# Softplus of a Mamba block by ScalarE's own function, in place of abs, relu, exp and ln summed by matmuls

## The chip, the cores and the metric

The kernel runs on one core of a Trainium2 chip. The metric is the device time of one execution in microseconds (us), as the median of the runs. A core has five engines that work side by side, each on its own instructions in their own order: TensorE (PE in the profile, with its weight loads as PEld), VectorE (DVE), ScalarE (ACT), GpSimd (POOL) and SyncE (SP), which here only issues transfers (DMAs). Engines wait for one another by semaphores. Tensors lie in SBUF; matmuls write to PSUM, which has eight banks of 128 partitions x 512 fp32 values.

## The reference

The input is 64 channels x 256 times x 128 frequencies. Layer 0 is a bidirectional Mamba block, first along time (128 sequences of 256), then along frequency (256 sequences of 128), each with a forward and a backward direction `d`. Layer 1 is a convolutional LSTM. The change concerns `dt` of layer 0, which is the same in all four blocks (2 stages x 2 directions):

```python
x = silu(conv(x) + conv_b)
dt, Bm, Cm = split(x @ x_proj_w.T)
dt = softplus(dt @ dt_proj_w.T + dt_proj_b)
h = exp(dt * A) * h + dt * B * x      # scan over the sequence
y = (sum over states of h * C + x * Dp) * silu(z)
```

`dt` has 128 values (the inner channels) per token. There are 16 states per channel, so `h` has 2048 rows per token.

## The kernel before

A stage (`class Stage`) works through 64 chunks of 512 tokens; the two stages make 128 chunks. A chunk has 16 steps S (`run`, L686): for each direction eight steps, each with 2 x 128 of the 2048 rows of h, that is, 128 partitions x 1024 values. One step consists of

- `inputs` (L546): two products on TensorE that spread dt times x over the states into the tile `bx` (two PSUM banks, three such tiles), issued two steps ahead of the scan;
- `decays` (L561): ScalarE's exp of dt times A into `dA` (four buffers), also two steps ahead;
- `times_b` (L580): `bx` times B, on VectorE, or on GpSimd for the "swapped" steps 2, 5, 9 and 14 of each chunk, for which ScalarE has copied `bx` to `dA` (L570) and put the exp into `bx`;
- `recur` (L590): the scan, on VectorE;
- `outputs` (L608): h times C, on GpSimd;
- `add_up` (L613): in every second step, four matmuls on TensorE that fold the states into `y`, two steps behind the scan.

The order of the work is written out by hand: each engine executes its instructions in the order in which `run` issues them. Within a step S that order is: times_b(S+1), recur(S), gate, outputs(S-1), inputs(S+2), decays(S+2), then what the tables `HEAD` (from chunk 1) or `SECOND` (chunk 0) put at slot S, then skip and add_up(S-2) with the closing of the last chunk, then what they put at S + 0.5.

These tables say when the preparations for the next chunk are done: loading, the norm (`means`, `rms`, `normalise`), the projections of x and z with the short convolution (`project_x`, `project_z`), `silus`, `dt`, `B` and `C`. Slots are steps of the chunk under way; slot 16 is step 0 of the new chunk itself. At slot 5, `project_x` of direction 1 is followed by `silus`: ScalarE loads the table set of silu (L385), applies silu to x and z of both directions (L389) and loads the table set of exp and ln again (L390). Around it `decays` is issued for two steps at slot 5 and for none at slot 6 (L707).

All small matmul results of a stage (px, pz, pb, pv, pm, po, made) take turns in one single PSUM bank, the tile with the tag "mm" (`mm`, L301): a new one is written only when the former has been read.

Softplus before is max(v, 0) + log(1 + exp(-|v|)) in three parts. `softplus_a` (L392) has the product `pv` and, on ScalarE, Abs into e, Relu within pv and exp into e. `softplus_b` (L405) takes w = e + 1, its Ln, and 1 - w. `softplus_sum` (L414) adds e, 1 - w and lw to pv by three matmuls with the identity, since 1 - w corrects the rounding of e + 1; ScalarE copies the sum to `dt`. The bank is held from softplus_a to that copy. `dt_away` (L426) then writes dt to DRAM by four DMAs on SP's queue, from where `spread_dt` (L456) fetches it for each step, spread over the states, into seven buffers; `times_x` (L433) makes dt times x on GpSimd. `first` (L471) does all that for the first chunk of a stage, before the steps begin.

Of the kernel before, what the change touches and what calls it, by code (L numbers as in the profile page):

```python
# [29 lines left out]
F32 = mybir.dt.float32  # L30
BF16 = mybir.dt.bfloat16
AF = mybir.ActivationFunctionType
# [4 lines left out]
P = 128  # L37
# [9 lines left out]
NTOK = 512  # L47
# [15 lines left out]
SWAPPED = (2, 5, 9, 14, 18, 21, 25, 30)  # L63
EXP_AND_LN = "natural_log_exp_and_others"
SILU = "silu_and_others"
EDGES = (0, 1, LF - 2, LF - 1)


# [10 lines left out]
    (5, "project_x", 1),  # L79
    (5, "silus"),  # L80
    (7.5, "project_bc", 0),
    (8, "softplus_a", 0),
    (8.5, "softplus_b", 0),
    (8.5, "spread_bc", 0, 0),
    (10.5, "softplus_sum", 0),
    (10.5, "dt_away", 0),
    (11.5, "times_x", 0),
    (12, "spread_bc", 0, 1),
    (12, "spread_dt", 0, 0),
    (12, "spread_dt", 0, 1),  # L90
    (12.5, "project_bc", 1),
    (12.5, "spread_dt", 0, 2),
    (13, "softplus_a", 1),
    (13, "softplus_b", 1),
    (13.5, "spread_dt", 0, 3),
    (14.5, "spread_dt", 0, 4),
    (15, "softplus_sum", 1),
    (15.5, "dt_away", 1),
    (16, "spread_dt", 0, 5),
    (16.5, "spread_dt", 0, 6),  # L100
    (16.5, "spread_dt", 0, 7),
# [15 lines left out]
SECOND = tuple(  # L117
    (max(slot, 16), *step) for slot, *step in HEAD if step[0] == "spread_dt" and step[1:] > [0, 3]
) + (
    (14, "softplus_a", 1),  # L120
    (15, "softplus_b", 1),
    (15, "softplus_sum", 1),
    (15, "dt_away", 1),
    (16, "spread_bc", 1, 0),
    (16, "spread_bc", 1, 1),
# [4 lines left out]
class Mamba:  # L130
# [58 lines left out]
    def load(self, first):  # L189
        dma, d = self.nc.sync.dma_start, self.d  # L190
        if first:
            dma(out=self.win[:, 0], in_=d["in_proj"][:, 0])
            dma(out=self.cw[:, 0], in_=d["conv_w"][0].partition_broadcast(C))
            dma(out=self.cols, in_=d["cols"])
            dma(out=self.xdt, in_=d["dt_proj"])
            dma(out=self.Wbc, in_=d["x_proj_bc"])
        else:
            dma(out=self.win[:, 1:4], in_=d["in_proj"][:, 1:4])
            dma(out=self.cw[:, 1:4], in_=d["conv_w"][1:4].partition_broadcast(C))
            dma(out=self.lin, in_=d["lin_w"])  # L200
            dma(out=self.b, in_=d["lin_b"])
            dma(out=self.ow, in_=d["out_proj"])
# [55 lines left out]
class Stage:  # L258
# [98 lines left out]
    def shifted(self, px, i):  # L357
        nc, m, L = self.nc, self.m, self.L
        first, second = (3, 1) if i % 2 == 0 else (4, 6)
        nc.tensor.matmul(self.seqs(px), lhsT=m.G1[i], rhs=self.unp[:, :, first : first + L], start=True, stop=False)  # L360
        nc.tensor.matmul(self.seqs(px), lhsT=m.G2[i], rhs=self.unp[:, :, second : second + L], start=False, stop=True)  # L361
# [21 lines left out]
    def silus(self, ch):  # L383
        nc = self.nc
        nc.scalar.preload_act_table_set(SILU)  # L385
        for n in ("xs", "zs"):
            for d in range(2):
                t = self.at[n, ch, d]
                nc.scalar.activation(t, t, AF.Silu)  # L389
        nc.scalar.preload_act_table_set(EXP_AND_LN)  # L390

    def softplus_a(self, ch, d):  # L392


        nc, m, wk = self.nc, self.m, self.wk
        i = 2 * self.stage + d
        pv = self.mm("pv")
        nc.tensor.matmul(pv, lhsT=m.Wdt[i], rhs=self.at["xs", ch, d], start=True, stop=True)  # L398
        e = wk.tile([P, NTOK], F32, name="e", tag="e")
        nc.scalar.activation(e, pv, AF.Abs, bias=m.dtb[:, i : i + 1])  # L400
        nc.scalar.activation(pv, pv, AF.Relu, bias=m.dtb[:, i : i + 1])
        nc.scalar.activation(e, e, AF.Exp, scale=-1.0)  # L402
        self.at["e", d], self.at["pv", d] = e, pv

    def softplus_b(self, ch, d):  # L405
        nc, wk = self.nc, self.wk
        w = wk.tile([P, NTOK], F32, name="w", tag="w")
        lw = wk.tile([P, NTOK], F32, name="lw", tag="lw")
        nc.scalar.activation(w, self.at["e", d], AF.Identity, bias=1.0)
        nc.scalar.activation(lw, w, AF.Ln)  # L410
        nc.scalar.activation(w, w, AF.Identity, scale=-1.0, bias=1.0)  # L411
        self.at["w", d], self.at["lw", d] = w, lw

    def softplus_sum(self, ch, d):  # L414

        nc, pv = self.nc, self.at["pv", d]
        parts = [self.at[n, d] for n in ("e", "w", "lw")]
        for n, t in enumerate(parts):
            nc.tensor.matmul(  # L419
                pv, lhsT=self.m.ident, rhs=t, start=False, stop=n == len(parts) - 1, skip_group_check=True  # L420
            )
        dt = self.wk.tile([P, NTOK], F32, name="dt", tag="dt", bufs=2)
        nc.scalar.copy(dt, pv)  # L423
        self.at["dt", d] = dt

    def dt_away(self, ch, d):  # L426

        there = self.dram.tile([32, 2, 2, NTOK], F32, name="there", tag="there")
        for r in range(4):
            self.nc.sync.dma_start(out=there[:, r % 2, r // 2], in_=self.at["dt", d][32 * r : 32 * r + 32])  # L430
        self.at["there", ch, d] = there

    def times_x(self, ch, d):  # L433
        dtx = self.wk.tile([P, NTOK], F32, name="dtx", tag="dtx", bufs=3)
        self.nc.gpsimd.tensor_mul(dtx, self.at["dt", d], self.at["xs", ch, d])  # L435
        self.at["dtx", ch, d] = dtx

    def project_bc(self, ch, d):
# [32 lines left out]
    def first(self):  # L471


        nc, m = self.nc, self.m
        s, time = 2 * self.stage, self.time
        banks = [self.ps_bx.tile([P, 2, NTOK], F32, name="bx", tag="bx") for _ in range(3)]
        self.load(0)
        if time:
            m.load(True)
        self.squares(0)  # L480
        if time:
            m.shifts(0)
        self.means(0)
        self.rms(0)
        nc.scalar.preload_act_table_set(SILU)
        self.normalise_here()
        if time:
            m.dt(0, self.mm("pw"))
            m.load(False)
        x, z = {}, {}  # L490
        for d in range(2):
            x[d] = self.wk.tile([P, NTOK], F32, name="xs", tag="xs", bufs=3)
            z[d] = self.wk.tile([P, NTOK], F32, name="zs", tag="zs", bufs=4)
            self.at["xs", 0, d], self.at["zs", 0, d] = x[d], z[d]
        self.shifted(banks[0][:, 0], s)
        nc.scalar.activation(x[0], banks[0][:, 0], AF.Silu, bias=m.cb[:, s : s + 1])
        nc.scalar.preload_act_table_set(EXP_AND_LN)
        self.softplus_a(0, 0)
        if time:
            m.decay()  # L500
            m.spreads()
            m.gates(0)
            m.shifts(1)
            m.gates(1)
        self.softplus_b(0, 0)
        self.spare = [banks[0][:, 1]]
        self.project_bc(0, 0)
        self.spread_bc(0, 0, 0)
        self.softplus_sum(0, 0)
        self.dt_away(0, 0)  # L510
        self.times_x(0, 0)
        for n in range(4):
            self.spread_dt(0, 0, n)
            if n == 0:
                self.spread_bc(0, 0, 1)
        if time:
            m.dt(1, self.mm("pw"))
        self.shifted(banks[1][:, 0], s + 1)
        for d in range(2):
            self.gated(banks[1 + d][:, 1], s + d)  # L520
        nc.scalar.preload_act_table_set(SILU)
        nc.scalar.activation(x[1], banks[1][:, 0], AF.Silu, bias=m.cb[:, s + 1 : s + 2])
        for d in range(2):
            nc.scalar.activation(z[d], banks[1 + d][:, 1], AF.Silu)
        nc.scalar.preload_act_table_set(EXP_AND_LN)
        self.spare = [banks[2][:, 0]]
        self.project_bc(0, 1)
        if time:
            m.folds(self.mm("pf"))
            for i in (2, 3):  # L530
                m.shifts(i)
                m.gates(i)
                m.dt(i, self.mm("pw"))
            for n in range(2):
                m.residual(n)
            for i in range(4):
                m.closing(i, self.mm("pc"))
# [274 lines left out]
class ConvLstm:  # L812
# [35 lines left out]
    def prepare(self):  # L848
        nc, tc, X, d, acc = self.nc, self.tc, self.X, self.d, self.acc
        g = self.gates.gb[:, 0:1]  # L850
        with tc.tile_pool(name="l_prep", bufs=1) as wp, tc.tile_pool(
# [28 lines left out]
            def border(wts, e, half, qs):  # L880

                tiles = []
                for gate in range(2):
                    pe = ps.tile([P, HALF, 2], F32, name="pe", tag="pe")
                    for q in qs:
                        x = EDGES[e] + q - 2
                        nc.tensor.matmul(  # L887
# [148 lines left out]
    def convolve_a(self, group, pair):  # L1036
# [6 lines left out]
        for e in range(2):  # L1043
            nc.scalar.copy(
                pre[:, :, :, EDGES[2 * e] : EDGES[2 * e] + 2],
                self.gxe[:, 2 * pair : 2 * pair + 2, half, rows, 2 * e : 2 * e + 2],
# [216 lines left out]
```

## Time and profile before

| | |
|---|---|
| time, median of 3 runs | 7332.51 us (7311.43 to 7338.29) |
| profiled execution, first to last instruction | 7324.0 us |
| stage along time, then along frequency, by the trace | about 0 to 3260 us and 3260 to 6550 us |
| ConvLSTM, by the trace | about 6550 us to the end |
| VectorE busy | 6924.8 us (95%) |
| GpSimd busy | 6703.3 us (92%) |
| TensorE busy | 6510.4 us (89%) |
| ScalarE busy | 6119.2 us (84%) |
| DMA engines busy, mean from 100 to 3200 us | 84% |

A line of the profile's groups names the code line (L598 is line 598), the engine, the operation, the tile written and the tile read, their shapes and the number of instructions; then the busy time in us, the mean of one instruction in ns, and the time that the engine stood idle just before such instructions, with what ended most of that. A line of the timeline has the start in us, the duration, the engine, the line and the operation with its count; what stands in brackets at its end is the idle time before it and the instruction whose end released it. Instructions of one engine overlap by about 0.1 us, and fp32 matmuls are shown in two passes.

### The profile page before, as it was taken

The page shows a single profiled execution, that of the slowest core. Times are in us where ns is not written, and L with a number is a line of the kernel's source. Part 1 is how long each engine was busy: PE and PEld are TensorE (multiplying, and loading weights), DVE is VectorE, ACT ScalarE, POOL GpSimd, SP SyncE. Part 2 cuts the span into 40 slices and gives each one's busy share as a digit, 9 for nine tenths or more (in the row PEclk, how much of TensorE's full clock was granted, in tenths as well). Part 3 has the DMA queues.
Part 4 walks back from the last instruction along what each step waited for, and adds up shares of the span by engine and source line. Part 5 has one row for each costly group of instructions (what it writes and reads, how often), then busy time and mean ns, then how long its engine had stood idle before and what let it go on. Part 6 is the DMA issues. An engine that isn't in the chain of part 4 may idle for free. (4 is left out here: it accounts for less than half of the span.)

```text
span 7324.0 us, 86482 instructions
## 1 busy us (share of the span) xinstructions
PE 6510.4 (89%) x25104; PEld 2254.8 (31%) x25104; DVE 6924.8 (95%) x4684; ACT 6119.2 (84%) x11092; POOL 6703.3 (92%) x3410
## 2 busy tenths in 40 slices
PE   8888888888888888887898898888888888888999
PEld 2222222222222222222222222222222222226887
DVE  7999999999999999997999999999999999996887
ACT  7888889888898888987999999988998989983333
POOL 6999999999999999997999999999999999995554
PEclk9999999999999999999999999999999999999999
DMA  7888888888888888886888888878888788882000
GB/s 171 206 206 208 199 210 204 205 207 205 210 203 209 206 204 207 204 210 159 208 211 209 210 215 200 208 197 202 206 201 204 199 209 198 205 202 62 15 15 17
DMA packets 505887, 1359.47 MB, mean 186 GB/s; under 512 B 72772, under 2 KB 129732, under 8 KB 505416
## 3 DMA queue, kind: packets, MB, share of 16 engines
q1 hardware_dynamic: 505416, 1353.93, 74.6%
q8 instruction: 205, 3.36, 0.2%
q14 instruction: 266, 2.18, 0.1%
HBM read 1228.34 MB, written 92.27 MB: 180 GB/s over the span
## 5 line engine op out<-in xcount | busy, mean ns | idle before, releaser
L611 POOL TENSOR_TENSOR h<-h,C 128x1024 f32<-128x1024 f32 x2048 | 4797.5, 2366 | 32.4 <-DVE h L598 22.0
L598 DVE TENSOR_TENSOR_SCAN h<-dA,bx 128x1024 f32<-128x1024 f32 x1536 | 3443.8, 2269 | 0.0
L553 PE MATMUL bx<-dtx,sel 64*128 64x512 f32 x8192 | 2578.7, 653 | 364.8 <-DVE h L598 362.5
L588 DVE TENSOR_TENSOR bx<-bx,B 128x1024 f32<-128x1024 f32 x1536 | 1863.7, 1213 | 178.8 <-PE bx L553 178.2
L576 ACT ACTIVATE dA<-rep,cols 128x510 f32<-128x510 f32 (+1 forms) x3072 | 2021.7, 710 | 11.3 <-DMA rep<-there 11.3
L585 POOL TENSOR_TENSOR dA<-dA,B 128x1024 f32<-128x1024 f32 x512 | 1205.9, 2355 | 161.9 <-ACT dA L570 155.8
L553 PEld LDWEIGHTS bx<-dtx,sel 64*128 64x128 f32 x8192 | 733.3, 190 | 1888.1 <-issue 1070.5
L620 PE MATMUL y<-h,fold 128*32 128x512 f32 x8192 | 1239.5, 618 | 12.6 <-POOL h L611 10.9
L598 DVE TENSOR_TENSOR_SCAN h<-bx,dA 128x1024 f32<-128x1024 f32 x512 | 1167.9, 2281 | 15.4 <-POOL dA L585 15.4
L570 ACT COPY dA<-bx 128x1024 f32<-128x1024 f32 x512 | 518.5, 1013 | 352.7 <-PE bx L553 338.0
L576 ACT ACTIVATE bx<-rep,cols 128x510 f32<-128x510 f32 (+1 forms) x1024 | 705.5, 689 | 33.7 <-ACT bx L573 0.4
L398 PE MATMUL pv<-xs,wdt 128*128 128x512 f32 x512 | 341.2, 753 | 261.5 <-ACT bc L443 167.5
L620 PEld LDWEIGHTS y<-h,fold 128*32 128x32 f32 x8192 | 188.5, 109 | 933.5 <-issue 504.0
L435 POOL TENSOR_TENSOR dtx<-dt,xs 128x512 f32<-128x512 f32 x256 | 327.6, 1280 | 54.2 <-ACT dt L423 33.7
L364 PE MATMUL pz<-unp,wz 64*128 64x512 f32 x504 | 283.5, 642 | 91.0 <-ACT X L669 54.0
L360 PE MATMUL px<-unp,g 128*128 128x512 f32 x504 | 283.8, 644 | 9.5 <-DMA unp<-xn 7.0
L419 PE MATMUL pv<-e,ident 128*128 128x512 f32 x512 | 288.1, 645 | 3.4 <-ACT e L402 3.4
L441 PE MATMUL pb<-xs,wbc 128*32 128x512 f32 x504 | 260.9, 599 | 15.6 <-ACT made L809 15.6
L419 PE MATMUL pv<-w,ident 128*128 128x512 f32 x512 | 262.6, 594 | 6.1 <-ACT w L411 6.1
L419 PE MATMUL pv<-lw,ident 128*128 128x512 f32 x512 | 262.3, 594 | 0.0
L361 PE MATMUL px<-unp,g 128*128 128x512 f32 x504 | 257.8, 592 | 0.0
L1150 POOL TENSOR_TENSOR y<-v,X 128x512 f32<-128x512 f32 x32 | 40.6, 1270 | 230.7 <-DVE v L1148 230.7
(206 smaller groups left out, 7066.0 us busy)
## 6 DMA issues: line engine op xcount, KB each, us to landing
rep<-there SPq DMA_DIRECT2D x2048, 512.0 KB, 7.8
B<-away SPq DMA_DIRECT2D x256, 256.0 KB, 8.9
there<-dt SPq DMA_DIRECT2D x1024, 64.0 KB, 3.3
C<-away SPq DMA_DIRECT2D x256, 256.0 KB, 3.4
unp<-xn SPq DMA_DIRECT2D x504, 64.0 KB, 3.3
away<-bc SPq DMA_DIRECT2D x256, 64.0 KB, 4.1
u<-in_x SPq DMA_DIRECT2D x128, 64.0 KB, 8.9
out<-y SPq DMA_DIRECT2D x32, 256.0 KB, 2.0
```

The costliest lines, as they stand in the source:

```text
L360: nc.tensor.matmul(self.seqs(px), lhsT=m.G1[i], rhs=self.unp[:, :, first : first + L], start=True, stop=False)
L398: nc.tensor.matmul(pv, lhsT=m.Wdt[i], rhs=self.at["xs", ch, d], start=True, stop=True)
L419: nc.tensor.matmul(pv, lhsT=self.m.ident, rhs=t, start=False, stop=n == len(parts) - 1, skip_group_check=True)
L435: self.nc.gpsimd.tensor_mul(dtx, self.at["dt", d], self.at["xs", ch, d])
L553: self.nc.tensor.matmul(bx[:, j], lhsT=self.m.sel[rows, r, k], rhs=dtx[rows], start=True, stop=True)
L570: nc.scalar.copy(dA.rearrange("p j n l -> p j (n l)"), bx)
L576: nc.scalar.activation(dA[:, j, :, live], self.seqs(rep[:, j])[:, :, live], AF.Exp, scale=m.A[:, i, g : g + 1])
L585: self.nc.gpsimd.tensor_mul(bx, bx, b)
L588: self.nc.vector.tensor_mul(bx, bx, b)
L598: self.nc.vector.tensor_tensor_scan(h.rearrange("p j n -> p (j n)")[:, step], dA[:, step], bx[:, step], 0.0, ALU.mult, ALU.add,)
L611: self.nc.gpsimd.tensor_mul(h, h, self.at["C", ch, d].unsqueeze(1).to_broadcast([P, 2, NTOK]))
L620: nc.tensor.matmul(y[32 * r : 32 * r + 32], lhsT=m.fold[:, k], rhs=hs[r % 2][:, r // 2], start=False, stop=k == NK - 1, skip_group_check=True,
```

## The change

Softplus becomes one ScalarE function, read from PSUM with the bias and written to `dt`. It needs a table set of its own, "softplus". For all chunks but a stage's first, both directions are done within `silus`, at slot 5: the product pv of direction 0 (`step_size`) is issued behind the silu of its x; after the four silus come the load of the new table set, `softplus` of direction 0, the product pv of direction 1, its softplus, and the load of the exp and ln set. The steps softplus_a, softplus_b and softplus_sum leave the tables; `dt_away` moves from slots 10.5 and 15.5 (15 in chunk 0) to 8 and 14.5 (15 in chunk 0, as before). `dt` gets three buffers in place of two. In `first`, the softplus of direction 0 and what follows from it come right behind its silu, with a table load more, and direction 1 is done behind the silus of the second half.

```diff
@@ HEAD
     (5, "project_x", 1),
     (5, "silus"),
     (7.5, "project_bc", 0),
-    (8, "softplus_a", 0),
-    (8.5, "softplus_b", 0),
     (8.5, "spread_bc", 0, 0),
-    (10.5, "softplus_sum", 0),
-    (10.5, "dt_away", 0),
+    (8, "dt_away", 0),
     (11.5, "times_x", 0),
...
     (12.5, "project_bc", 1),
     (12.5, "spread_dt", 0, 2),
-    (13, "softplus_a", 1),
-    (13, "softplus_b", 1),
     (13.5, "spread_dt", 0, 3),
     (14.5, "spread_dt", 0, 4),
-    (15, "softplus_sum", 1),
-    (15.5, "dt_away", 1),
+    (14.5, "dt_away", 1),
@@ SECOND
-    (14, "softplus_a", 1),
-    (15, "softplus_b", 1),
-    (15, "softplus_sum", 1),
     (15, "dt_away", 1),
@@ silus
                 nc.scalar.activation(t, t, AF.Silu)
+                if n == "xs" and d == 0:
+                    self.step_size(ch, 0)
+        nc.scalar.preload_act_table_set(SOFTPLUS)
+        self.softplus(ch, 0)
+        self.step_size(ch, 1)
+        self.softplus(ch, 1)
         nc.scalar.preload_act_table_set(EXP_AND_LN)
 
-    def softplus_a(self, ch, d):
...
-    def softplus_b(self, ch, d):
...
-    def softplus_sum(self, ch, d):
...
+    def step_size(self, ch, d):
+        i = 2 * self.stage + d
+        self.at["pv", d] = pv = self.mm("pv")
+        self.nc.tensor.matmul(pv, lhsT=self.m.Wdt[i], rhs=self.at["xs", ch, d], start=True, stop=True)
+
+    def softplus(self, ch, d):
+        i = 2 * self.stage + d
+        dt = self.wk.tile([P, NTOK], F32, name="dt", tag="dt", bufs=3)
+        self.nc.scalar.activation(dt, self.at["pv", d], AF.Softplus, bias=self.m.dtb[:, i : i + 1])
+        self.at["dt", ch, d] = dt
@@ first
         nc.scalar.activation(x[0], banks[0][:, 0], AF.Silu, bias=m.cb[:, s : s + 1])
+        nc.scalar.preload_act_table_set(SOFTPLUS)
+        self.step_size(0, 0)
+        self.softplus(0, 0)
+        self.dt_away(0, 0)
+        self.times_x(0, 0)
         nc.scalar.preload_act_table_set(EXP_AND_LN)
-        self.softplus_a(0, 0)
...
-        self.softplus_b(0, 0)
         self.spare = [banks[0][:, 1]]
         self.project_bc(0, 0)
         self.spread_bc(0, 0, 0)
-        self.softplus_sum(0, 0)
-        self.dt_away(0, 0)
-        self.times_x(0, 0)
...
         for d in range(2):
             nc.scalar.activation(z[d], banks[1 + d][:, 1], AF.Silu)
+        nc.scalar.preload_act_table_set(SOFTPLUS)
+        self.step_size(0, 1)
+        self.softplus(0, 1)
         nc.scalar.preload_act_table_set(EXP_AND_LN)
```

More of the change, by code (lines that the diff above doesn't have):

```diff
@@ L65 @@
 SILU = "silu_and_others"
+SOFTPLUS = "softplus"
 EDGES = (0, 1, LF - 2, LF - 1)
@@ L389, in silus @@
                 nc.scalar.activation(t, t, AF.Silu)
+                if n == "xs" and d == 0:
[4 more added lines that the diff above has]
+        self.softplus(ch, 1)
         nc.scalar.preload_act_table_set(EXP_AND_LN)
-    def softplus_a(self, ch, d):
-        nc, m, wk = self.nc, self.m, self.wk
+    def step_size(self, ch, d):
         i = 2 * self.stage + d
[L397 to L403, printed above, removed]
-    def softplus_b(self, ch, d):
[L406 to L412, printed above, removed]
-    def softplus_sum(self, ch, d):
[L416 to L424, printed above, removed]
+        self.at["pv", d] = pv = self.mm("pv")
[5 more added lines that the diff above has]
+        self.at["dt", ch, d] = dt
     def dt_away(self, ch, d):
@@ L429, in dt_away @@
         for r in range(4):
-            self.nc.sync.dma_start(out=there[:, r % 2, r // 2], in_=self.at["dt", d][32 * r : 32 * r + 32])
+            self.nc.sync.dma_start(out=there[:, r % 2, r // 2], in_=self.at["dt", ch, d][32 * r : 32 * r + 32])
         self.at["there", ch, d] = there
@@ L434, in times_x @@
         dtx = self.wk.tile([P, NTOK], F32, name="dtx", tag="dtx", bufs=3)
-        self.nc.gpsimd.tensor_mul(dtx, self.at["dt", d], self.at["xs", ch, d])
+        self.nc.gpsimd.tensor_mul(dtx, self.at["dt", ch, d], self.at["xs", ch, d])
         self.at["dtx", ch, d] = dtx
```

## The prediction

> **What bounds the kernel now.** I read the page's busy shares first, then its groups, then the answer on who waited for whom, and last the timeline of one chunk. The groups say who works without pause:
>
> ```profile
> L611 POOL TENSOR_TENSOR h<-h,C 128x1024 f32<-128x1024 f32 x2048 | 4797.5, 2366 | 32.4 <-DVE h L598 22.0
> L598 DVE TENSOR_TENSOR_SCAN h<-dA,bx 128x1024 f32<-128x1024 f32 x1536 | 3443.8, 2269 | 0.0
> L588 DVE TENSOR_TENSOR bx<-bx,B 128x1024 f32<-128x1024 f32 x1536 | 1863.7, 1213 | 178.8 <-PE bx L553 178.2
> ```
>
> VectorE's scans (3443.8 + 1167.9), products with B (1863.7) and gates (170.2) make 6645.6 us for 128 chunks: 51.9 us each as single durations, about 50 us as they overlap by 0.1 us. A chunk takes 51.6 us in the trace (one chunk's swapped scan of step 2 starts at 2004.30, the next one's at 2055.89). From 110 to 3200 us VectorE waits 73.5 us in all for TensorE, 1.2 us a chunk. So in the two Mamba stages a microsecond that VectorE loses is lost, and one that other engines save is not won unless it shortens that wait. GpSimd, as full, follows VectorE and regains nothing for it.
>
> What feeds VectorE is TensorE's product `bx`, issued two steps ahead into three buffers, in one program order with everything else on TensorE. The timeline of one chunk around the silus (start, duration, engine, line):
>
> ```profile
> 1606.09 1.02 PE L361 MATMUL px<-unp,g 128*128 128x512 f32 x2
> 1607.04 1.06 PE L620 MATMUL y<-h,fold 128*32 128x512 f32 x8
> 1607.53 0.67 ACT L373 ACTIVATE xs<-px,cols 128x512 f32<-128x512 f32 x1
> ...
> 1608.04 1.13 PE L553 MATMUL bx<-dtx,sel 64*128 64x512 f32 x4
> 1608.21 1.28 ACT L385 ACT_TABLE_LOAD   x1
> 1609.51 1.15 ACT L389 ACTIVATE xs<-xs 128x512 f32<-128x512 f32 x2
> 1609.82 1.21 DVE L588 TENSOR_TENSOR bx<-bx,B 128x1024 f32<-128x1024 f32 x1
> ...
> 1610.56 1.13 ACT L389 ACTIVATE zs<-zs 128x512 f32<-128x512 f32 x2
> 1611.71 1.28 ACT L390 ACT_TABLE_LOAD   x1
> ...
> 1616.22 2.08 PE L398 MATMUL pv<-xs,wdt 128*128 128x512 f32 x2 [1.83 <-ACT bc L443]
> 1618.23 1.81 PE L553 MATMUL bx<-dtx,sel 64*128 64x512 f32 x4
> 1619.97 1.06 PE L620 MATMUL y<-h,fold 128*32 128x512 f32 x8
> 1620.09 1.23 DVE L588 TENSOR_TENSOR bx<-bx,B 128x1024 f32<-128x1024 f32 x1 [1.32 <-PE bx L553]
> ```
>
> The reader is to see two things. At 1607.04 TensorE goes straight from px to add_up(3) and the inputs of step 8, which end at 1609.17, only 0.65 us before VectorE takes them at 1609.82. And at 1616.22 the pv product of softplus_a, behind ScalarE's bc copy in the one shared PSUM bank, holds up the next inputs: VectorE stands for 1.32 us. That is today's whole stall in the chunk, and it is a small copy of what the change sets up.
>
> **What the Trainium skill says.** "ScalarE: Activation LUTs", What ACT_TABLE_LOAD costs: a switch costs 1283 ns plus a drain of 1380. The trace agrees with the first (126 loads, mean 1283) and not with the second: the load at 1608.21 follows an activation that ended at 1608.20, and the next starts 0.02 after it. The same page (the end of Step-by-step) says that all functions cost the same per element, and its price for a [128,1] bias, 280 + 0.833 x 512, makes 707 ns for Softplus; no Softplus is in the trace, but the Abs that reads pv with the same bias takes 682 (L400), and I take that. "TensorE: Matmul & The Clock Gate", Part 1, says that matmuls run at half rate after an idle window and for about 3.4 us of work; the trace agrees: after 1.83 us of idleness the pair at 1616.22 takes 2.08 us against 1.12 for the same pair at 1631.94, and matmuls are quick again 3.75 us later. The same page, Part 2, step 1, says that matmuls stay in program order; the order above is that of the code.
>
> **The change, part by part.** Removed on ScalarE, per direction: Abs, Relu, two Identities, Exp, Ln, and the copy of dt. Their seven rows sum to 1132 us over the span. Added: 256 Softplus at 0.68 (175 us) and 126 third table loads at 1.28 (162 us). Removed on TensorE: the identity sums of L419, three rows (288 + 263 + 262 = 813 us). All this is off VectorE's path, hidden behind its 50 us a chunk; it can return at most the 1.2 us of waiting. I credit 0.8 us: the waits come from pv at step 10 (1.3 in the chunk shown) and from px at step 1 (0.33), which both lose their cause, but a TensorE with more gaps starts cold more often, so some wait stays. Without that credit the change costs 0.8 us more a chunk.
>
> The move is the costly part. The matmuls pv0 and pv1 now sit inside silus, at slot 5, between px1 and add_up(3). pv0 needs silu(xs0). pv1 needs the bank that pv0 holds, so it waits for softplus 0, behind three more silus and a table load. Behind pv1 on TensorE stand add_up(3) and inputs(8); VectorE waits for inputs(8), and GpSimd's and ScalarE's step 9 behind it. From the rows above:
> - ScalarE: silu table 1608.21, silus 1609.51 to 1611.69, Softplus table in the place of today's second load (1611.71 to 1612.99), softplus 0 to 1613.68. pv0 runs from about 1610.15 to 1612.2, cold, and is in time.
> - TensorE: pv1 starts at 1613.73. Idle for all but 2 of the 6.6 us since 1607.1, it is cold: step of 1.92 to the next group (two cases, 2.01 at 1616.22 and 1.83 at 2025.62), so 1615.65.
> - add_up(3): 1.00 from its start to the next group's when warm; cold 1.95, as an estimate, by the ratio of inputs cold to warm (2.08 and 2.00 against 1.13). So 1617.60.
> - inputs(8): 3.87 after TensorE's restart, so warm: 1.13, to 1618.73.
> VectorE starts at 1618.76 in place of 1609.82: 8.94 us lost. In the second stage's chunk at 5060 the same px1 eviction starts at 5065.64 and VectorE wants the product 2.01 later (2.29 in the first), so 9.22. Mean 9.1. ScalarE itself, with softplus 1 (to 1616.4) and the last table load (to 1617.7), is free before inputs(9) exist (1619.8), so its added load costs nothing beyond the stall; if that cover went, it would cost its 1.28.
>
> Bounds for what the trace lacks: all warm, pv1 + add_up + inputs take 1.06 + 1.00 + 1.13 and VectorE starts at 1616.95, a stall of 7.1 to 7.4; all cold, 2.0 + 1.95 + 2.08, 9.9 to 10.2. A Softplus of 0.60 or 1.0 shifts it by -0.1 or +0.3.
>
> The rest: dt_away is issued at slot 8, ahead of the B spread, so four DMAs (1.7 to 3.0 us of SP's queue) go before it; B is first needed at step 16, some 24 us later, so nothing. dt_away 1 goes one slot earlier, with dt long ready, past one rep load (wanted steps later): nothing; SP's queue then has no late dt to stand on. The third dt buffer lets dt of a new chunk be written before times_x of slot 20.5: it avoids a wait. In `first` each stage has dt about 5.7 us sooner (23.84 against about 18.1) but pays a table load, a pv1 and a softplus in the second direction (about 3.5); the first VectorE product hangs on the load of u behind these. Zero, within 5 us each.
>
> Sum: (9.1 - 0.8) x 126 chunks = 1046 us. On the profiled span of 7324.0 that is 8370. The median of the runs, 7332.5, is 8.5 above that span; with the same distance I forecast 8380 us.
>
> **Rivals.** Warm TensorE: the clock stays up, (7.25 - 1.2) x 126 = 762 us, 8095. For it: gaps of 1.2 us are followed by full speed (1630.87). Against: these gaps are 3.1 and 1.5 with little between. Chance 0.15.
>
> Worse than one stall: TensorE remains cold behind it and ScalarE's copy for the swapped step 9, GpSimd's product and the scan come late too, 10.0 + 0.5 with no credit: 10.5 x 126 = 1323, 8655. Against: VectorE has two scans (7 and 8) to do meanwhile. Chance 0.15.
>
> The other side: ScalarE, relieved of some 6 us a chunk ((1132 - 175 - 162) / 128), runs ahead and does the block before TensorE needs inputs(8), so only the 1.2 us is won: 7332 - 150 = 7180. It decides where TensorE's standing at pv0 and pv1 sums to under 0.65 us; the eviction, two table loads, silus and softplus between px1 and pv1 alone are 6.1 (1607.53 to 1613.68). Also, ScalarE already waits for bx before step 5's copy (1.10 at 1599.61; 338 us in all), so it is tied to VectorE there and cannot be ahead. Chance 0.03. That the new function leaves the order unchanged, with pv not in TensorE's way, would be the same within 0.5%: 0.01.
>
> **How the numbers follow.** My forecast has 0.66. The range is 8110 to 8610: the low end near the warm case, the high one (8610 - 7332) / 126 = 10.1 us a chunk, the cold bound without credit; it leaves out part of the outer cases and both small ones, some 0.2. A change of 0.5% is about what a measurement of this kernel can tell from none. Faster 0.03, same 0.01, slower 0.96.
>
> **What would show it.** VectorE's wait at L588 for L553 from 178 us to about 1150 plus, near 9 us once a chunk and right after px1; VectorE's busy time unchanged near 6925, its share near 83%; TensorE waiting for silu and softplus (about 3 and 1.5 to 3 us a chunk); the pv1 pair near 2 us; a third group of 126 table loads at 1.28; ScalarE busy near 5320; the ConvLSTM's stretch unchanged. I would be wrong if the stall by itself were under 7 or over 10.5 us, if table loads showed a drain, or if the VectorE gap came at another step.

## The result, and the profile after

The changed kernel takes 8194.3 us (median, 8192.5 to 8196.7) against 7335.4 us before (the runs of the table above and one more): a ratio of 1.118, 95% interval 1.116 to 1.119. It is 859 us slower. The forecast was 8380 us in a range of 8110 to 8610. The profiled execution has a span of 8194.9 us, 870.9 more than the profile before.

The groups of the changed kernel's page that answer to those shown of before (busy us, mean ns | idle time before them and what ended it):

```profile
L591 POOL TENSOR_TENSOR h<-h,C 128x1024 f32<-128x1024 f32 x2048 | 4791.8, 2361 | 163.4 <-DVE h L578 131.9
L578 DVE TENSOR_TENSOR_SCAN h<-dA,bx 128x1024 f32<-128x1024 f32 x1536 | 3449.8, 2275 | 0.0
L568 DVE TENSOR_TENSOR bx<-bx,B 128x1024 f32<-128x1024 f32 x1536 | 1866.2, 1215 | 1081.0 <-PE bx L533 1080.8
```

VectorE does the same work in about the same time (6904.1 us busy against 6924.8). What grew is one number: its wait for TensorE's `bx`, from 178.2 to 1080.8 us, 902.6 us more. The scans of swapped steps, which had waited 15.4 us for GpSimd, no longer wait. So the whole loss stands in this one wait. From 110 to 3200 us of the trace it occurs 53 times in all and sums to 440.6 us: 8.31 us, once a chunk, and nowhere else. Over both stages it is, by the timeline, 1053 us in 126 chunks, 8.36 us each; the other 28 us belong to the starts of the two stages. Steps are counted here by the scan that a product is for; this wait is that of step 8.

The timeline of the changed kernel around the silus of one chunk (start, duration, engine, line, in us):

```profile
1632.64 1.02 PE L353 MATMUL px<-unp,g 128*128 128x512 f32 x2
...
1634.09 0.67 ACT L365 ACTIVATE xs<-px,cols 128x512 f32<-128x512 f32 x1
1634.69 2.29 DVE L578 TENSOR_TENSOR_SCAN h<-dA,bx 128x1024 f32<-128x1024 f32 x1
1634.78 1.28 ACT L377 ACT_TABLE_LOAD   x1
1636.07 1.15 ACT L381 ACTIVATE xs<-xs 128x512 f32<-128x512 f32 x2
1636.76 1.77 PE L394 MATMUL pv<-xs,wdt 128*128 128x512 f32 x2 [3.09 <-ACT xs L381]
1637.13 1.14 ACT L381 ACTIVATE zs<-zs 128x512 f32<-128x512 f32 x2
1638.29 1.28 ACT L384 ACT_TABLE_LOAD   x1
1639.58 0.69 ACT L400 ACTIVATE dt<-pv,cols 128x512 f32<-128x512 f32 x1
1640.32 2.07 PE L394 MATMUL pv<-xs,wdt 128*128 128x512 f32 x2 [1.79 <-ACT dt L400]
1642.32 1.84 PE L600 MATMUL y<-h,fold 128*32 128x512 f32 x8
1642.43 0.69 ACT L400 ACTIVATE dt<-pv,cols 128x512 f32<-128x512 f32 x1 [2.16 <-PE pv L394]
1643.14 1.28 ACT L388 ACT_TABLE_LOAD   x1
1644.09 1.99 PE L533 MATMUL bx<-dtx,sel 64*128 64x512 f32 x8
1645.27 1.23 DVE L568 TENSOR_TENSOR bx<-bx,B 128x1024 f32<-128x1024 f32 x1 [8.29 <-PE bx L533]
```

The reader is to follow TensorE from px1 on. It stands 3.09 us for silu of x0 and 1.79 us for softplus 0; between and after these it runs pv0, pv1 and the fold of add_up(3) at about half rate; and only then come the inputs of step 8, which VectorE has wanted since its scan ended at 1637.0. Over the run, TensorE's waits at these two places sum to 390.4 and 212.4 us in 126 chunks each, 3.10 and 1.69 us a chunk. Its mean granted clock fell from 0.975 to 0.889 of full speed.

### The profile page after: what moved, and what is told of

Its sections match the earlier page's. It is cut to its first block, busy times and chain, and to the rows that moved or that the text cites. A ratio compares the mean times of both kernels' runs of the same rounds, so it can differ in the third digit from the quotient of the medians.

```text
span 8194.9 us, 82165 instructions
## 1 busy us (share of the span) xinstructions
PE 6387.5 (78%) x23568; PEld 2104.4 (26%) x23568; DVE 6904.1 (84%) x4684; ACT 5424.3 (66%) x9686; POOL 6699.0 (82%) x3410
## 5 line engine op out<-in xcount | busy, mean ns | idle before, releaser
L533 PE MATMUL bx<-dtx,sel 64*128 64x512 f32 x8192 | 2626.5, 683 | 1075.5 <-DVE h L578 1064.9
L568 DVE TENSOR_TENSOR bx<-bx,B 128x1024 f32<-128x1024 f32 x1536 | 1866.2, 1215 | 1081.0 <-PE bx L533 1080.8
L533 PEld LDWEIGHTS bx<-dtx,sel 64*128 64x128 f32 x8192 | 767.5, 200 | 2711.9 <-issue 1886.0
L600 PE MATMUL y<-h,fold 128*32 128x512 f32 x8192 | 1440.8, 750 | 10.3 <-POOL h L591 8.6
L550 ACT COPY dA<-bx 128x1024 f32<-128x1024 f32 x512 | 518.8, 1013 | 931.4 <-PE bx L533 914.1
L394 PE MATMUL pv<-xs,wdt 128*128 128x512 f32 x512 | 503.5, 1086 | 604.3 <-ACT xs L381 390.4
L612 ACT ACTIVATE y<-xs,cols 128x512 f32<-128x512 f32 x256 | 177.6, 694 | 663.6 <-DVE yz L616 663.6
L400 ACT ACTIVATE dt<-pv,cols 128x512 f32<-128x512 f32 x256 | 176.4, 689 | 275.2 <-PE pv L394 273.6
L394 PEld LDWEIGHTS pv<-xs,wdt 128*128 128x128 f32 x512 | 113.8, 277 | 900.5 <-ACT xs L381 494.8
```

Source lines behind the costliest of these rows:

```text
L394: self.nc.tensor.matmul(pv, lhsT=self.m.Wdt[i], rhs=self.at["xs", ch, d], start=True, stop=True)
L533: self.nc.tensor.matmul(bx[:, j], lhsT=self.m.sel[rows, r, k], rhs=dtx[rows], start=True, stop=True)
L550: nc.scalar.copy(dA.rearrange("p j n l -> p j (n l)"), bx)
L568: self.nc.vector.tensor_mul(bx, bx, b)
L600: nc.tensor.matmul(y[32 * r : 32 * r + 32], lhsT=m.fold[:, k], rhs=hs[r % 2][:, r // 2], start=False, stop=k == NK - 1, skip_group_check=True,
```

## The experiments

The theory: the loss is the place of pv0 and pv1 in TensorE's order, ahead of the inputs that VectorE needs next. The rivals: A, the table switches or the new function cost more than their rows; B, ScalarE's longer block delays its exps. A third question was how much the half clock adds. The kernel before, measured beside these runs, took 7322 to 7324 us.

**The wait alone.** Two matmuls with unused results are put into the kernel before; there is no Softplus function and no third load.

```diff
                 nc.scalar.activation(t, t, AF.Silu)
+                if (n, d) in (("xs", 0), ("zs", 1)):
+                    nc.tensor.matmul(self.mm("idle"), lhsT=self.m.Wdt[0], rhs=t, start=True, stop=True)
         nc.scalar.preload_act_table_set(EXP_AND_LN)
```

> The kernel before with two additional matmuls in the silus, at the place where the change has pv0 and pv1: one reads x of direction 0 behind its silu, the other z of direction 1 behind the last silu. Their results are not used; no Softplus function, no third table load. Theory: TensorE stands from the end of px1 until silu x0, runs the first cold (2.0), then the second (2.0), add_up(3) and inputs(8): some 6.7 us later than before, with nearly all of today's other waits kept: 7335 + 126 x 6.7 = 8180 us, range 8000 to 8250. Rival A (table loads or the Softplus function cost the time) and rival B (ScalarE's longer block delays its exps): both are absent here, so 7335 to 7450 us.

Measured: 8163.1 us, ratio 1.114 (1.112 to 1.117). The timeline of this kernel:

```profile
2029.32 0.67 ACT L373 ACTIVATE xs<-px,cols 128x512 f32<-128x512 f32 x1
2029.43 2.27 DVE L600 TENSOR_TENSOR_SCAN h<-dA,bx 128x1024 f32<-128x1024 f32 x1
...
2031.99 1.13 PE L391 MATMUL idle<-xs,wdt 128*128 128x512 f32 x2 [3.08 <-ACT xs L389]
2033.55 2.08 PE L391 MATMUL idle<-zs,wdt 128*128 128x512 f32 x2 [0.43 <-ACT zs L389]
2035.55 1.72 PE L622 MATMUL y<-h,fold 128*32 128x512 f32 x8
2037.20 1.99 PE L555 MATMUL bx<-dtx,sel 64*128 64x512 f32 x8
2038.38 1.23 DVE L590 TENSOR_TENSOR bx<-bx,B 128x1024 f32<-128x1024 f32 x1 [6.67 <-PE bx L555]
```

Two matmuls that wait for ScalarE at this place cost 840 us, with the arithmetic of softplus as before. Neither rival is in this kernel, nor are the earlier `dt_away` and the third `dt` buffer. VectorE stands at the same product as in the changed kernel. The chunk shown, with 6.67 us, is a mild one, since the first extra pair ran at full rate; over the 126 chunks this wait sums to 959 us, 7.61 us a chunk, against 8.36 in the changed kernel. The expectation came as near as it did by two errors that cancel: it had 6.7 us a chunk, and it kept nearly all of the old waits, of which the one at step 11 went.

**ScalarE's order kept, TensorE's mended.** In the changed kernel the Softplus block moves from slot 5 to 6. ScalarE runs the same instructions in the same order; pv0 and pv1 come after inputs(8).

```diff
     (5, "silus"),
+    (6, "softplus_both"),
...
+    def softplus_both(self, ch):
+        nc.scalar.preload_act_table_set(SOFTPLUS)
+        for d in range(2):
+            self.step_size(ch, d)
+            self.softplus(ch, d)
+        nc.scalar.preload_act_table_set(EXP_AND_LN)
```

> The changed kernel with the block of Softplus load, pv0, softplus 0, pv1, softplus 1 and exp load moved from slot 5 to slot 6. ScalarE's order stays exactly that of the changed kernel; on TensorE pv0 and pv1 now come behind add_up(3) and inputs(8) instead of ahead of them. Theory: VectorE has step 8 in time; inputs(9) and (10) then stand behind pv1 and step 10's product is about 5.2 us late: 7335 + 126 x (5.2 - 1.2) = 7840 us, range 7600 to 7950. Rival B (ScalarE's block of three loads, four silus and two softplus is what costs): the same as the changed kernel, 8190 us.

Measured: 7826.2 us, ratio 1.069 (1.067 to 1.071), 14 us from the theory's figure. The timeline of this kernel shows step 8 served in time and the next wait where the theory has it, at step 10, behind pv1. It is 4.39 us in the chunk shown and 5.43 us in the mean of the 126 chunks, where 5.2 was estimated:

```profile
2035.34 1.21 DVE L570 TENSOR_TENSOR bx<-bx,B 128x1024 f32<-128x1024 f32 x1
...
2038.53 1.12 PE L396 MATMUL pv<-xs,wdt 128*128 128x512 f32 x2 [2.43 <-ACT dt L402]
...
2045.30 1.23 DVE L570 TENSOR_TENSOR bx<-bx,B 128x1024 f32<-128x1024 f32 x1 [4.39 <-PE bx L535]
```

Rival B falls: with ScalarE's instructions in unchanged order 368 us are back.

**One direction only.** Direction 1 is taken out of the silus; its pv, load, softplus and load come at slot 13.

```diff
+    (13, "softplus_one", 1),
...
         self.softplus(ch, 0)
-        self.step_size(ch, 1)
-        self.softplus(ch, 1)
         nc.scalar.preload_act_table_set(EXP_AND_LN)
```

> The changed kernel with direction 1 taken out of the silus: pv1, Softplus load, softplus 1 and exp load come at slot 13 (its dt leaves at 15.5), direction 0 stays as changed. Theory: TensorE stands only at pv0 (about 3.1 us, then pv0, add_up(3) and inputs(8) at half clock), so VectorE's wait falls from 8.3 to about 5 us a chunk: 7325 + 126 x (5.0 - 1.2) = 7800 us, range 7650 to 7950. There are five table loads a chunk in place of three: if the loads or ScalarE's time were the cost, it would be slower than the changed kernel (8194 us) by 126 x 1.28 x 2 = 320 us.

Measured: 7670.3 us, ratio 1.048 (1.046 to 1.049): faster than the changed kernel by 524 us with two more loads a chunk. VectorE's wait for bx is 556.5 us in the whole run, 4.2 us a chunk at step 8 (expected: about 5). The wait for pv1, with what follows it, is thus about half of the stall: (1080.8 - 556.5) / 126 = 4.2 us a chunk, more than TensorE's 1.69 of standing and the 2.07 of pv1 itself by 0.4.

**A table load more.** In the kernel before, the Softplus set is loaded and replaced at once.

```diff
                 nc.scalar.activation(t, t, AF.Silu)
+        nc.scalar.preload_act_table_set(SOFTPLUS)
         nc.scalar.preload_act_table_set(EXP_AND_LN)
```

> The kernel before with one more table load in the silus: the Softplus set is loaded and at once replaced by the exp and ln set. Nothing else is changed. Theory (the loss is TensorE standing at pv0 and pv1, in front of the inputs of step 8): 126 loads at 1.28 us; ScalarE's copy for the swapped step 9 comes 1.28 us later, GpSimd's product and the scan of step 9 with it, so between nothing and 1.2 us a chunk, 7335 to 7490 us. Rival A (the table switch is what costs, with a drain that the rows don't show, 2.7 us or more each): 7335 + 126 x 2.6 = 7660 us or more, and over 7900 if it is to explain most of the 859 us.

Measured: 7546.8 us, ratio 1.030 (1.029 to 1.032). This is outside both figures, nearer to the theory: 223 us for 126 loads, 1.77 us each. The groups and the waits of this kernel:

```profile
L391 ACT ACT_TABLE_LOAD x126 | 161.7, 1283 | 2.3
L392 ACT ACT_TABLE_LOAD x126 | 161.7, 1283 | 0.7
```

```profile
DVE bx L590 <- PE bx L555: 258.5, 249, 22.8
DVE h L600 <- POOL dA L587: 150.7, 110, 3.8
```

The load itself takes 1.28 us and no idle time follows it. Against the kernel before, VectorE's wait at the swapped scans grew from 15.4 to 150.7 us (ScalarE's copy comes later, so GpSimd's product does) and the one for bx from 178.2 to 258.5. Both together are 216 of the 223 us. A load that is late by 1.28 us was passed on more than once; I had counted the swapped step 9 alone. Behind the silus ScalarE had no such slack in the kernel before, but in the changed kernel VectorE's stall covers the same load: ScalarE itself waits for bx there, 1.70 us at 1646.12 (its copy at L550).

**TensorE kept busy.** In the changed kernel five matmuls a chunk add zeros to y, three ahead of pv0, two ahead of pv1.

```diff
+        self.add_nil(3)
         for n in ("xs", "zs"):
...
                     self.step_size(ch, 0)
+        self.add_nil(2)
         nc.scalar.preload_act_table_set(SOFTPLUS)
...
+    def add_nil(self, times):
+        for _ in range(times):
+            self.nc.tensor.matmul(
+                self.y, lhsT=self.m.ident, rhs=self.nil, start=False, stop=False, skip_group_check=True)
```

> The changed kernel with five more matmuls per chunk that add a tile of zeros to y: three ahead of pv0, two between pv0 and pv1, so that TensorE works through its two waits. y stays what it was. Theory with the half clock as a part of the stall (pv1 2.0, add_up 1.8 and inputs up to 2.0 for 1.06, 1.0 and 1.13): at full speed the stall is some 1.8 us shorter, 8194 - 126 x 1.8 = 7970 us. If the clock is no part of it: 8194 us or, where the added matmuls end late, a little more.

Measured: 7996.1 us, ratio to before 1.092 (1.090 to 1.094): 198 us less than the changed kernel, by adding work. The timeline of this kernel has pv1 and the fold at full rate:

```profile
2052.45 1.12 PE L404 MATMUL pv<-xs,wdt 128*128 128x512 f32 x2 [0.72 <-ACT dt L410]
2053.50 1.07 PE L610 MATMUL y<-h,fold 128*32 128x512 f32 x8
2054.50 1.99 PE L543 MATMUL bx<-dtx,sel 64*128 64x512 f32 x8
2055.68 1.23 DVE L578 TENSOR_TENSOR bx<-bx,B 128x1024 f32<-128x1024 f32 x1 [6.79 <-PE bx L543]
```

The half rate was 1.6 us of the 8.4 us a chunk (198 / 126; expected: 1.8); pv1 fell from 2.07 to 1.12 and the fold from 1.84 to 1.07, 1.7 together.

**The function in the old places.** Silus as before; at slots 8 and 13 one direction each.

```diff
+    (8, "softplus_one", 0),
...
-    (8, "dt_away", 0),
+    (10.5, "dt_away", 0),
...
+    (13, "softplus_one", 1),
...
-    (14.5, "dt_away", 1),
+    (15.5, "dt_away", 1),
...
+    def softplus_one(self, ch, d):
+        self.step_size(ch, d)
+        self.nc.scalar.preload_act_table_set(SOFTPLUS)
+        self.softplus(ch, d)
+        self.nc.scalar.preload_act_table_set(EXP_AND_LN)
```

> The new function kept, its place put back: silus as before, and at slots 8 and 13 for one direction each pv, Softplus load, softplus, exp load, in place of softplus_a and softplus_b; dt leaves at 10.5 and 15.5 as before. Six table loads a chunk. Theory: ScalarE's block of 3.3 us stands where 3.8 us of the seven functions stood, TensorE is rid of the three sums; VectorE's wait behind pv0 at step 11 (1.3 us) stays, the small one at step 3 (0.33 us) goes: 7325 - 126 x 0.3 = 7290 us, range 7200 to 7380. Rival A (table switches cost more than their rows): four loads more than before, 504 in all, each 1.3 us or more on the path: 7980 us or more.

Measured: 7143.8 us, ratio 0.976 (0.975 to 0.977): faster than both kernels, with six table loads a chunk. Rival A falls with it. The gain is larger than expected: VectorE's wait behind pv0 at step 11 went too. TensorE stands 1.09 us ahead of pv0 in place of the 1.83 of the chunk shown of before, and pv0 runs at full rate, 1.13 us in place of 2.08:

```profile
2009.85 1.13 PE L396 MATMUL pv<-xs,wdt 128*128 128x512 f32 x2 [1.09 <-ACT bc L422]
```

In the second version direction 0 stands one slot later, at 9.

> As v1_slots, with direction 0's block at slot 9 instead of 8, so that pv0 stands behind inputs(11) instead of ahead of them. Theory: VectorE's wait of 1.3 us at step 11 goes as well, and VectorE works almost without a pause: 7325 - 126 x 1.2 = 7170 us, range 7120 to 7260, faster than both kernels. If pv0's place did not matter: the same as v1_slots.

Measured: 7133.0 us, ratio 0.974 (0.973 to 0.976). VectorE's waits for bx are 30.4 us in the whole run, 19.2 of it a single one at the change of stages, so the Mamba stages now run at VectorE's own pace. The place of pv0 was worth 11 us here and not 1.0 us a chunk, since the wait it was to take away had gone already.

**Why the waits of before went.** Two runs put load back into the version with slots 8 and 13: TensorE's (three matmuls a direction that add zeros to y, at 9.5 and 15) and ScalarE's (two unused copies a direction).

```diff
+    (9.5, "more", 0),
...
+    (15, "more", 1),
...
+    def more(self, ch, d):
+        for _ in range(3):
+            self.nc.tensor.matmul(
+                self.y, lhsT=self.m.ident, rhs=self.nil, start=False, stop=False, skip_group_check=True)
```

> v1_slots with TensorE's old load put back: at slots 9.5 and 15 three matmuls each add a tile of zeros to y, as many as the sums that the change removed; they wait for no other engine's softplus. It asks why v1_slots gained 178 us where some 40 were expected, VectorE's wait at step 11 having gone too. If TensorE's sums were what made TensorE late in the kernel before: about 7300 us. If it is ScalarE's relief (it comes to the silus and to the bc copy 0.7 us earlier, so that pv0 starts after 1.1 us of idleness, at full clock, instead of 1.8): about 7145 to 7180 us.

```diff
+    (10.5, "more", 0),
...
+    (15, "more", 1),
...
+    def more_of(self, ch, d):
+        t = self.wk.tile([P, NTOK], F32, name="more", tag="more")
+        self.nc.scalar.copy(t, self.at["xs", ch, d])
...
         self.step_size(ch, d)
+        self.more_of(ch, d)
         self.nc.scalar.preload_act_table_set(SOFTPLUS)
...
+    def more(self, ch, d):
+        t = self.wk.tile([P, NTOK], F32, name="more", tag="more")
+        self.nc.scalar.copy(t, self.at["dt", ch, d])
```

> v1_slots with ScalarE's old load put back in about its old places: for each direction a copy of x ahead of the Softplus load and a copy of dt at slots 10.5 and 15, 1.2 us together, into a tile that is not used. If ScalarE's relief made the gain: back to about 7250 to 7330 us, with VectorE waiting at step 11 again. If TensorE's removed sums made it: about 7145 to 7180 us.

Measured: 7408.5 us (ratio 1.012, 1.010 to 1.013) with TensorE's load, 7192.9 us (0.982, 0.981 to 0.984) with ScalarE's. Neither meets a figure that was expected. VectorE's waits, two lines of the first kernel and one of the second (without load the wait for bx is 38.2 us):

```profile
DVE bx L580 <- PE bx L545: 161.1, 315, 19.7
DVE yz L628 <- PE y L411: 86.5, 125, 1.5
```

```profile
DVE bx L581 <- PE bx L546: 84.3, 102, 17.5
```

The wait for bx with TensorE's load, 161.1 us, seems to be the 178.2 of before. Sorted by step over the whole timelines, without the starts of the two stages, it is so only in part (us):

| kernel | step 3 | step 10 | step 11 | step 12 | steps 15 and 0 |
|---|---|---|---|---|---|
| before | 47.5 | 5.6 | 86.4 | 0 | 0 |
| slots 8 and 13 | 0.4 | 0.3 | 8.0 | 0 | 1.7 |
| with TensorE's load | 41.8 | 5.5 | 35.3 | 47.9 | 1.1 |
| with ScalarE's load | 0 | 0 | 1.6 | 0 | 54.7 |

TensorE's load brings back the waits at steps 3 and 10 and part of the one at step 11. ScalarE's brings back none of them and makes new ones at steps 15 and 0. The pauses of TensorE ahead of pv0 say the same: 1.7 us or more 106 times before, 4 times with slots 8 and 13, 105 times with TensorE's load and once with ScalarE's. So, as far as these runs show, the old waits went because TensorE was relieved. That ScalarE's relief had a part, by its earlier bc copy, is not shown.

The kernel with TensorE's load is even slower than the one before. In part this is because the added matmuls stand ahead of the gate, which reads y, and of the inputs of step 12; the sums stood behind both, at slot 10.5:

```profile
2033.87 1.12 PE L400 MATMUL pv<-xs,wdt 128*128 128x512 f32 x2 [1.83 <-ACT bc L432]
...
2038.31 3.12 PE L411 MATMUL y<-nil,ident 128*128 128x512 f32 x6
2041.36 1.99 PE L545 MATMUL bx<-dtx,sel 64*128 64x512 f32 x8
2041.47 0.69 DVE L628 TENSOR_TENSOR yz<-y,zs 128x512 f32<-128x512 f32 x1 [1.53 <-PE y L411]
2042.54 1.23 DVE L580 TENSOR_TENSOR bx<-bx,B 128x1024 f32<-128x1024 f32 x1 [0.38 <-PE bx L545]
```

These two waits, 86.5 and 47.9 us, are costs of the experiment and may shift what follows them. So the two runs show which engine's load matters and not what share of the 178 us each part is worth. Why half of the wait at step 11 stayed away stays open as well: after pauses as long as before, pv0 ran at full rate more often (82 of 105 times, against 43 of 106).

## Why the prediction was right, and where it was off

- **What bounds the kernel**: right. VectorE's busy time did not move, and its added waits (902.6 - 15.4 = 887 us) less 21 us of busy time are 866 of the 871 us of span.
- **What is removed is off the path**: right in the changed kernel. ScalarE's busy time fell by 695 us and TensorE's by 123, and neither shortened anything but VectorE's small waits. ScalarE's 5424 us are above my 5320, mostly since I summed single durations that overlap.
- **The place and chain of the stall**: right, step by step. From the start of px1's eviction to VectorE's start I had 11.23 us (1607.53 to 1618.76); the trace has 11.18 (1634.09 to 1645.27) and, in the second stage, 11.00 (5614.37 to 5625.37). The step of pv1 was put at 1.92 and is 2.00, the fold's at 1.95 and is 1.77. The wait-alone kernel shows the mechanism without the function.
- **The size of the stall, 9.1 us**: the term that was mis-sized; it measured 8.4. The chain had its length, but VectorE came later to it: it wants the product 2.79 us after that eviction started (1636.88; 2.61 in the second stage, both medians of 63 chunks), not 2.29 and 2.01 as in the kernel before. I took from the old trace how far ScalarE is ahead of VectorE at slot 5 and held it fixed, though the change itself unloads ScalarE and TensorE before that slot. The wait-alone kernel, which has the stall but all of the old work, confirms this: there it is 2.28 and 1.99 as before (2029.32 to 2031.6 in the chunk shown), so it was the removed work that moved it and not the stall. Over 126 chunks this is (9.1 - 8.36) x 126 = 93 us.
- **The credit of 0.8 us for the old waits**: too small. All are gone, about 1.31 us a chunk ((178.2 + 15.4 - 28) / 126, 28 being what is left beside the 126 stalls). The caution that a colder TensorE keeps some of them was not needed. This is another 65 us. With the first and VectorE's 21 us less of busy time it makes 179 us, where the forecast span of 8370 was 175 above the measured one. The forecast time was 186 high: I had added the 8.5 us by which the median stood above the span before, and rounded up, while the new median stands 0.6 below its span.
- **ScalarE's third load costs nothing beyond the stall**: borne out by ScalarE's own wait for bx behind it (1.70 us at 1646.12). Its price without cover, given as 1.28, was 1.77.
- **The rivals**: the warm one's time, 8095, is nearer to the measured 8194 than my 8380, so the number alone would speak for it. The trace doesn't: pv1 and the fold ran at half rate, 2.07 and 1.84 us where they take 1.12 and 1.07 with TensorE kept busy. My figure was high by the two terms above, not by the clock. Of what the clock is worth the rival had about the right idea (1.85 us a chunk of the 9.1; 1.6 measured). The cold-throughout one (8655) fails, as inputs(8) ran at full rate. The one on the other side (7180) was excluded for the reason given. Yet the same function at another slot passes its time of 7180 (7143.8): the change had that gain in it and placed it where it could not be had.
- **The clock**: that pv1 would be cold held, with 2.07 us at 1640.32. The reading that the trace agrees with a rule of idle windows goes too far. The pause of 1.83 us ahead of the slow pair at 1616.22 is followed by full rate elsewhere in the same kernel (last section).

## What to carry to other kernels

On an engine that works in order, a matmul that waits for another engine holds up everything behind it: before placing one, look at which instruction behind it feeds the bounding engine next and how many tenths of a microsecond that one has to spare (0.65 us here, against 6 us of waiting). Put such a matmul behind the urgent one, where its own operand is long ready, and count a restart at half rate as part of the wait. The same cheaper function was worth 2.6% or cost 11.8% here, by where it stood; and when a change relieves engines ahead of the disputed place, the slack read from the old trace moves as well.

## What the runs showed of the hardware that was not expected

- Softplus from PSUM with a bias column takes 689 ns for 128x512 fp32, close to Abs with the same operands (682), and the switch to its set 1283 ns like all others (126 to 504 extra loads), with the next activation 0.01 to 0.02 us behind it. No drain beside it was seen in these traces, against what the Trainium skill has ("ScalarE: Activation LUTs", What ACT_TABLE_LOAD costs).
- Adding matmuls of zeros, five a chunk, made the changed kernel 198 us faster.
- The length of a pause does not by itself tell whether the matmuls behind it run slow. In the wait-alone kernel the first extra pair follows the same pause of 3.1 us in 117 chunks (from 100 us on, by the timeline); in 107 it took about 2.1 us and in 10, as at 2031.99, 1.1. In the kernel before, of 106 pv0 pairs behind a pause of 1.7 us or more, 43 ran at full rate, 43 at half (2.0 us or more) and the others between. The 21 behind less than 1.25 us all ran at full rate, as did the 82 of the version with slots 8 and 13.
